# Eight chained layers on one core: edge tokens moved into the first query block, pieces placed between score passes, the two heads' probability tiles side by side, and one block of the last FFN beside the attention

## The chip, the cores and the metric

The kernel runs on one NeuronCore of a Trainium2 chip, as one launch. The metric is the time of that launch on the device in microseconds (us). Matrix products run on TensorE (PE in the profile, with its weight loads as PEld), sums, maxima and reads of PSUM on VectorE (DVE), activations on ScalarE (ACT), some elementwise work on GpSimd (POOL), and SyncE (SP) issues the DMAs.

## The reference, cut to what matters

The input is 2048 tokens of width 128. Four attention layers and four FFN layers follow each other, each as `x = x + f(layernorm(x))`:

```python
x = x + _L0_attn_ref(...)   # 16 heads of 8, softmax over all 2048 tokens
x = x + _L0_ffn_ref(...)    # 512 wide, gelu
x = x + _L1_attn_ref(...)   # 16 heads of 64, softmax over all 2048 tokens
x = x + _L1_ffn_ref(...)    # silu(x wg) * (x wu), 384 wide
x = x + _L2_attn_ref(...)   # each token sees its left and right neighbour and itself, in a ring
x = x + _L2_ffn_ref(...)    # 8 experts, the best one
x = x + _L3_attn_ref(...)   # a memory of two 32x32 matrices, updated in chunks of 64 tokens
x = x + _L3_ffn_ref(...)    # 8 experts of 176, the best two, and a shared one
```

Three things in this matter for the change. The second attention (L1) needs a row maximum and a row sum over 2048 keys for every query and head. The third (L2) needs the key and value of the neighbours of each token, so a block of 256 tokens needs one token of each neighbouring block. The fourth (L3) is sequential: each of its 32 chunks of 64 tokens starts from the state that the chunk before it left.

## The kernel before

The work stands in two long stretches and an end.

The first stretch is the L0 attention, with the L0 FFN and the keys and values of L1 worked in. The change leaves its order alone.

The second is the L1 attention (`l1_attn`, line 1070 on). Its 2048 queries are cut into five query blocks, `QB`, each as (first token, tokens, columns): 512, 384, 512, 384 and 256 tokens. For each block there are eight pairs of heads; a block and a pair make a **unit**, 40 units in all, worked in the order of the blocks. A unit goes over 16 key tiles of 128 keys. One key tile is: four score passes for each of the two heads (a product with the high part of q, one with its low part, one with the low part of the keys, one that adds the negative row maximum), the exponential of both heads' scores on ACT into tiles `P`, and the product of `P` with the values, which comes one key tile late. The sums over keys are not taken from TensorE: `do_sum` adds up the tiles `P`, on POOL (`acg`) for key tiles 0 to 13 and on DVE (`acd`) for 14 and 15, each head by itself, and `do_merge` adds the two. At the end of the unit `u_end` sums these over the partitions, takes the reciprocal, scales, and after every second pair multiplies with Wo (`stage_wo`). Row maxima of later units are made ahead of time (`u_max`): products of q tiles with 512 keys (`km`), reduced on DVE (`mx`).

The layers after L1's attention run as **pieces** beside it. Each stage is a generator that yields between pieces: `stage_a` (L1 FFN), `stage_a2` and `stage_b` (L2 attention), `stage_b2` (L2 FFN), `stage_c`, `chunk` and `stage_d` (L3 attention), `stage_g`, `stage_e0`, `s_lane` and `stage_e1` (L3 FFN). They work on blocks of 256 tokens, eight in all; `c` and `d` on 128, `chunk` on 64. L3's FFN has 13 groups of hidden units for each block of 256, so 104 groups. A planner (`Part.may`, `fill`, line 176 on) decides while the program is written, by a cost for each instruction, which piece can go in; `fill` is called twice for each key tile. The result is one fixed order for each engine. What a yield says matters: an integer over 0 asks for so many PSUM banks, "T" says that the piece begins with a product on TensorE; with `only="t"` `fill` takes neither of these kinds.

`stage_b` of any block waits for `stage_m`, which carries three single **edge tokens** (1280, 1792 and 2047) through the L1 FFN. They ride as extra columns in the second query block, `(512, 384, 388)`, and so come out with unit 15. `stage_a` of a block waits for the query block that holds it.

The third stretch, here the **end**, is what the pieces have left when the 40 units are done. Five more lanes for the FFN are opened there, and all remaining banks. L3's FFN adds its 13 groups for a block up in one PSUM bank, `ac`, which it holds from `stage_e0` to `stage_e1`.

Of the kernel before, what the change touches and what calls it, by code (L numbers as in the profile page):

```python
# [20 lines left out]
D = 128  # L21
# [10 lines left out]
T = dict(lead0=22, more0=4, mgap=0.4, pvq=2, lim0=0.5, fq=(3,), pl=-0.5, pr=1.0, tlow=2, tback=3, late=0.3, pvp="mx", mxp="mx", ex=(1280, 1792, 2047), low=1, lows='ge', keep=1, leave=2, pvn=1, sp=0, rdy=40., eu=2, qg=(22, 16, 10), em=2, el=6, sem=0.2, same=1.2, tsame=3.0, order="hdmBbAaEcCeg", ps=dict(st=3, mx=5), dma=2.3, slack=0.1, lim=0.3, backlog=2.5, lead=(10, 8, 6), pp=7, dve=(14, 15), qp=(1, 1), lanes=2, xl=5,  # L32
         QB=[(0, 512, 512), (512, 384, 388), (896, 512, 512), (1408, 384, 384), (1792, 256, 256)])

# [36 lines left out]
def body(ctx: ExitStack, tc: tile.TileContext, x, pa, pb, pc, pi, pd, pr, pr0, pe, pw, out):  # L71
# [90 lines left out]
    pp = ctx.enter_context(tc.tile_pool(name="pp", bufs=T["pp"]))  # L162
# [31 lines left out]
    class Part:  # L194
# [24 lines left out]
        def step(self):  # L219
            piece[0] = clk["T"]  # L220
            r = next(self.gen, "end")
            self.same = r == "same"
            self.ready = 0.0 if self.same else piece[0] + (r if type(r) is float else 0.0)
            self.pe = r == "T"
            self.banks = r if type(r) is int else 0
            self.seen = len(emitted) if r is False else -1
            if r == "end":
                emitted.add(self.key)
            return r != "end"
# [140 lines left out]

    QB = T["QB"]
    EXTRA = T['ex']
    units = [(qb, p) for qb in range(len(QB)) for p in range(NP1)]
    qhh, qfs, kmx, mx1 = {}, {}, {}, {}

    qx = [mid.tile([128, 8], F32R, name=f"qx{i}") for i in range(2)]
    xq = {}

    def u_loadx(qb):
        t0, tn, n = QB[qb]  # L380
        xq[qb] = l1x.tile([128, 512], F32, name="xq", tag="xq", bufs=2)
        if n != tn:
            ge.memset(xq[qb][:, tn:n], 0.0)
            for i, t in enumerate(EXTRA):
                sy.dma_start(xq[qb][:, tn + i:tn + i + 1], xnd[:, t:t + 1])
        sy.dma_start(xq[qb][:, :tn], xnd[:, t0:t0 + tn])

    def u_qprep(u):
        qb, p = units[u]
        if qb not in xq:  # L390
            u_loadx(qb)
        n = QB[qb][2]
        yield 1
        ps = mi()
        mm(ps[:, :n], C("wq", p * 128, 128), xq[qb][:, :n])
        yield
        qf = l1x.tile([128, 512], F32, name="qf", tag="qf")
        se.activation(qf[:, :n], ps[:, :n], AF.Identity, bias=bq8[:, p:p + 1], scale=0.125)
        rel(ps)
        yield  # L400
        qhh[u] = l1q.tile([128, 512], F32R, name="qh", tag="qh")
        se.copy(qhh[u][:, :n], qf[:, :n])
        yield
        qfs[u] = qf
        tn, n = QB[qb][1:]
        if n > tn:
            for e in range(2):
                r = slice(64 * e, 64 * e + 64)
                se.copy(qx[u % 2][r, 4 * e:4 * e + n - tn], qf[r, tn:n])
# [15 lines left out]
    def u_max(u, i):  # L425
# [8 lines left out]
        if 128 * qt == tn:  # L434
            ps = amx()
            mm(ps[0:8], qx[u % 2], kmx[(u, c)])
            ve.tensor_reduce(mx1[u][0:8, 0, 3, c:c + 1], ps[0:8], AX.X, ALU.max)
            rel(ps)
            return 1
# [9 lines left out]
    def u_maxend(u):  # L449
# [6 lines left out]
        if n > tn:  # L456
            ve.tensor_reduce(m[0:8, 0, 3:4], mx[0:8, 0, 3, :], AX.X, ALU.max)
        yield 1
        t = mi()
        if n > tn:  # L460
            te.transpose(t[0:1, 256:264], m[0:8, 0, 3:4], ident[0:8, 0:8])
# [5 lines left out]
        if n > tn:  # L467
            for e in range(2):
                se.mul(mbt[u % 2][64 * e:64 * e + 1, tn:n], t[0:1, 256 + 4 * e:256 + 4 * e + n - tn], -1.0)
# [50 lines left out]
    l0w = l0ctx.enter_context(tc.tile_pool(name="l0w", bufs=2))  # L520
    qd = dram.tile([16, 6, 8, S], BF16, name="qd")
# [150 lines left out]
    def l0_attn():  # L672
# [49 lines left out]
        for g in range(N):  # L722
# [9 lines left out]
            for q in range(4):  # L732
# [17 lines left out]
                p = pp.tile([128, 512], F32, name="P", tag="P")  # L750
# [202 lines left out]
    leave[0] = T["leave"]  # L953
# [10 lines left out]
    l1a = ctx.enter_context(tc.tile_pool(name="l1a", bufs=2, reuse_waits="tile"))  # L964
# [11 lines left out]
    def u_end(u, o, accs):  # L976
# [4 lines left out]
        if u == len(units) - 1:  # L981
            for e in range(2):
                mm(t[64 * e:64 * e + 64, :n], ones[:, 0:64], accs[e][:, :n], par=(e == 1))
# [8 lines left out]
        for e in range(2):  # L992
            mm(t[32 * e:32 * e + 32, :n], ones[:, 0:32], accs[e][:, :n], tile_position=(0, 32 * e), par=(e == 1))
# [29 lines left out]
    def stage_wo(qb, part):  # L1023
# [4 lines left out]
        for p in range(2 * part, 2 * part + 2):  # L1028
            mm(ps[:, :n], C("wo", p * 128, 128), O.pop(p)[:, :n], start=(p % 2 == 0), stop=(p % 2 == 1))
            yield  # L1030
        if part == 0:
            w = l1w.tile([128, 512], F32, name="wac", tag="wac", bufs=1)
# [9 lines left out]
        del wacc[qb]  # L1042
        yield 1
# [9 lines left out]
        if n != tn:  # L1053
            ne = len(EXTRA)
            xm = edge_x[0] = sm.tile([ne, 128], F32, name="xm", tag="xm", bufs=1)
            for i, t in enumerate(EXTRA):
                sy.dma_start(xm[i:i + 1, :], xs[t % 128:t % 128 + 1, t // 128, :])
# [8 lines left out]
    def l1_attn():  # L1066
        LEAD = dict(zip((256, 384, 512), T["lead"]))
        LEAD.update({260: LEAD[384], 388: LEAD[512]})
# [13 lines left out]
        def do_pv(g, pts, v):  # L1082
            u, k = divmod(g, 16)
            n = QB[units[u][0]][2]
            if k == 0:
                pv[u] = take([T["pvp"]])
            for e in range(2):
                mm(pv[u][64 * e:64 * e + 64, :n], v[:, k % SPC, 64 * e:64 * e + 64], pts[e][:, :n],
                   start=(k == 0), stop=(k == 15), par=(e == 1))
            if k == 15:  # L1090
# [5 lines left out]
                rel(pv.pop(u))  # L1096
                ends.append((u, o, accs))

        def do_sum(g, pts, v):
            u, k = divmod(g, 16)  # L1100
            n = QB[units[u][0]][2]
            for e in range(2):
                a = acc.setdefault(u, [None, None])
                f = first.setdefault((u, e), {})
                eng, nm = (ve, "d") if k in T["dve"] else (ge, "g")
                if nm not in f:
                    f[nm] = [pts[e]]
                    continue
                if len(f[nm]) == 1:
                    if u:  # L1110
                        need(("s", u - 1), ("o", u - 1))
                    t = l1a.tile([128, 512], F32, name="ac" + nm, tag="ac" + nm)
                    eng.tensor_tensor(t[:, :n], f[nm][0][:, :n], pts[e][:, :n], ALU.add)
                    f[nm] = [t, 1]
                else:
                    t = f[nm][0]
                    eng.tensor_tensor(t[:, :n], t[:, :n], pts[e][:, :n], ALU.add)
                if k == 15:
                    a[e] = f["d"][0]
                    merge.append((f["d"][0], f["g"][0], n))  # L1120
                    del first[(u, e)]
# [3 lines left out]
        def do_merge():  # L1125
            while merge:
                d, g_, n = merge.pop(0)
                ve.tensor_tensor(d[:, :n], d[:, :n], g_[:, :n], ALU.add)
            while ends:
                u, o, accs = ends.pop(0)  # L1130
                helper(("o", u), u_end(u, o, accs), max(wr[tname(t)] for t in accs))
# [4 lines left out]
        for g in range(16 * U):  # L1136
# [6 lines left out]
            if u + 2 < U:  # L1143
                if k == 1 and units[u + 2][1] == 0:
                    need(("q", u + 1))
                    u_loadx(units[u + 2][0])
# [10 lines left out]
            pts = []  # L1157
# [3 lines left out]
            for i, (a, b) in enumerate(ops):  # L1161
                for e in range(2):
                    rows = slice(64 * e, 64 * e + 64)
                    mm(pss[e][:, :n], a[rows], b[rows, :n], start=(i == 0), stop=(i == 3), par=e and 0.02)
            for e in range(2):
                pt = pp.tile([128, 512], F32, name="P", tag="P")
                se.activation(pt[:, :n], pss[e][:, :n], AF.Exp)
                rel(pss[e])
                pts.append(pt)
            max_upto(max_at(g + 16 + LEAD[n] + 1))  # L1170
            fill()
            if prev:
                do_sum(*prev[-1])
            if len(prev) == T["pvn"]:
                while prev:
                    do_pv(*prev.pop(0))
                fill()
            do_merge()
# [135 lines left out]
    def stage_m():  # L1314
# [22 lines left out]
        xt = sm.tile([128, 4], F32, name="xtm", tag="xtm", bufs=2)  # L1337
        yield from norm_T(xt)
        h = sm.tile([128, 12], F32, name="hm", tag="hm", bufs=1)
        for k in range(3):  # L1340
# [4 lines left out]
            th = sm.tile([128, 4], F32, name="thm", tag="thm", bufs=2)  # L1345
# [3 lines left out]
            ve.scalar_tensor_tensor(h[:, 4 * k:4 * k + ne], th[:, :ne], 0.5, ps[:, 64:64 + ne], ALU.mult, ALU.mult)  # L1349
# [3 lines left out]
        for k in range(3):  # L1353
            mm(ps[:ne, :128], h[:, 4 * k:4 * k + ne], tok(wi, 6 + k), start=(k == 0), stop=(k == 2))
# [4 lines left out]
        xt = sm.tile([128, 4], F32, name="xtm", tag="xtm", bufs=2)  # L1359
        yield from norm_T(xt)  # L1360
        ps = mi()
        for i in range(2):
            mm(ps[:, 4 * i:4 * i + ne], tok(w2m, i), xt[:, :ne])
        yield
        for i in range(2):
            for j, t in enumerate(EXTRA):
                se.activation(edge[:, t // BN, i, int(t % BN > 0):int(t % BN > 0) + 1], ps[:, 4 * i + j:4 * i + j + 1],
# [258 lines left out]
    def chunk(b, c):  # L1626
# [49 lines left out]
        yield  # L1676
# [151 lines left out]
    def lane_tiles(lane):  # L1828
# [4 lines left out]
        if lane not in lane_bufs:  # L1833
            n = lane - LANES
            if n < 2:
                t = ("acd", "acg")[n]
                ws = [l1a.tile([128, 512], F32, name=t, tag=t)[:, :384] for _ in range(2)]
# [10 lines left out]
    def lane_work(lane):  # L1848
        if lane < LANES:
            return bt(f"t3{lane}", 1), bt(f"te{lane}", 1)  # L1850
        p = pp.tile([128, 512], F32, name="P", tag="P")
        return p[:, :BN], p[:, BN:]
# [19 lines left out]
    def stage_e0(b):  # L1872
        d = E[b]
        yield 1
        ac = mi()
        for i in range(BT):
            mm(tok(ac, i), tok(d["rT"][:, 0], i), pes[0:9, 128:256], start=(i == 0), stop=False)
        d["ac"] = ac

    def s_lane(lane):  # L1880

        q = []
        while ("l", NB_ - 1) not in emitted:
# [33 lines left out]
            yield T["late"]  # L1917
            d["left"] -= 1
            for i in range(BT):
                mm(tok(ac, i), tok(th[:nr], i), w[:nr, 2, :], start=False, stop=(d["left"] == 0 and i == BT - 1))  # L1920
            if d["left"] == 0:
# [3 lines left out]
    def stage_e1(b):  # L1925
        c0, ac = BT * b, E.pop(b)["ac"]
        add_tok(ac, c0)
        yield
# [69 lines left out]
    def s_e0():  # L1998
        for b in range(NB_):
            yield from wait(("g", b))  # L2000
            if b and not tail:
                yield from wait(("l", b - 1))
# [115 lines left out]
```

## Time and profile before

| | |
|---|---|
| median of three runs | 2989.47 us (2988.46 to 3006.5) |
| the profiled execution | 3001.08 us |
| its span, first to last instruction | 2999.2 us |
| first and last score pass of the L1 attention (PE, `mbt,onr`) | 908.6 and 2593.8 us |
| from there to the end of the span | 405 us |
| PE busy | 2769.9 us (92%) |
| DVE busy | 2194.9 us (73%) |
| ACT busy | 1582.9 us (53%) |
| POOL busy | 1522.3 us (51%) |
| granted TensorE clock, mean | 0.936 |

Busy time is the union of an engine's instructions. PE is counted busy from a matmul's start to its modelled end, so a PE busy to 100% can still have small gaps between its products; weight loads (PEld) lie beside it. Nearly every instruction has the line 147, that of the helper that records it, so the groups are told apart by the tiles that they write and read (out<-in).

### The profile page before, as it was taken

The page shows a single profiled execution, that of the slowest core. Times are in us where ns is not written, and L with a number is a line of the kernel's source. Part 1 is how long each engine was busy: PE and PEld are TensorE (multiplying, and loading weights), DVE is VectorE, ACT ScalarE, POOL GpSimd, SP SyncE. Part 2 cuts the span into 40 slices and gives each one's busy share as a digit, 9 for nine tenths or more (in the row PEclk, how much of TensorE's full clock was granted, in tenths as well). Part 3 has the DMA queues.
Part 4 walks back from the last instruction along what each step waited for, and adds up shares of the span by engine and source line. Part 5 has one row for each costly group of instructions (what it writes and reads, how often), then busy time and mean ns, then how long its engine had stood idle before and what let it go on. Part 6 is the DMA issues. An engine that isn't in the chain of part 4 may idle for free.

```text
span 2999.2 us, 49776 instructions
## 1 busy us (share of the span) xinstructions
PE 2769.9 (92%) x16719; PEld 1307.0 (44%) x16719; DVE 2194.9 (73%) x4699; ACT 1582.9 (53%) x3933; POOL 1522.3 (51%) x1762
## 2 busy tenths in 40 slices
PE   7999999999979899999999999899989898888998
PEld 2222222322234344454444444455544555565666
DVE  7899898898534666566666778887677769787765
ACT  1788887888854444444444444444434334333444
POOL 2400110201127688866776876677767556443444
PEclk9999999999979999999999999999999999776779
DMA  6311231321144333433442332233334343312244
GB/s 142 72 28 22 72 84 17 101 54 46 53 141 135 92 112 110 121 110 111 138 119 87 94 95 87 89 105 108 109 97 114 108 117 94 88 52 61 76 104 115
DMA packets 247749, 275.80 MB, mean 92 GB/s; under 512 B 95747, under 2 KB 183330, under 8 KB 247366
## 3 DMA queue, kind: packets, MB, share of 16 engines
q1 hardware_dynamic: 246630, 272.43, 33.2%
q8 instruction: 132, 2.16, 0.3%
q14 instruction: 123, 1.01, 0.1%
q10 hardware_dynamic: 864, 0.20, 0.0%
HBM read 229.97 MB, written 42.28 MB: 91 GB/s over the span
## 4 chain that ended last, share of the span: by engine, by line
PE 70%; DVE 18%; ACT 6%; issue 3%; DMA 3%; POOL 1%; SPq 0%; ACTq 0%; DVEq 0%; POOLq 0%
PE mi L147 70%; DVE mx L147 5%; ACT P L147 3%; DVE sB L147 1%; DVE o L147 1%; DVE gq L147 1%; DMA ka<-kvd 1%; DVE gt L147 1%; DVE xs L147 1%; ACT kf L147 1%; ACT kh L147 1%; DVE xn L147 1%; DVE sG L147 1%; DVE acd L147 1%; DVE sA L147 0%
## 5 line engine op out<-in xcount | busy, mean ns | idle before, releaser
L147 DVE TENSOR_REDUCE mx<-mi 128x1 f32<-128x512 f32 (+1 forms) x2080 | 1322.1, 683 | 582.8 <-PE mi L147 571.5
L147 ACT ACTIVATE P<-mi 128x512 f32<-128x512 f32 (+3 forms) x2304 | 1137.0, 551 | 1004.1 <-PE mi L147 973.2
L147 POOL TENSOR_TENSOR acg<-acg,P 128x512 f32<-128x512 f32 (+3 forms) x960 | 1011.4, 1083 | 181.8 <-ACT P L147 180.0
L147 PE MATMUL mi<-P,ka 128*64 128x512 f32 (+3 forms) x2560 | 597.6, 546 | 2.3 <-DVE mx L147 2.3
L147 PE MATMUL mi<-qh,ka 64*128 64x512 f32 (+3 forms) x2560 | 521.0, 406 | 9.7 <-DMA ka<-kvd 6.8
L147 PEld LDWEIGHTS mi<-qh,ka 64*128 64x128 f32 x2560 | 247.0, 189 | 382.5 <-issue 347.0
L147 PE MATMUL mi<-kop,qop 48*128 48x512 bf16 x1024 | 348.6, 405 | 24.5 <-DVE mx L147 12.1
L147 PE MATMUL mi<-qop,kop 50*128 50x512 bf16 x1024 | 317.8, 391 | 27.1 <-ACT P L147 24.7
L147 PE MATMUL mi<-P,vop 128*32 128x512 f32 x2048 | 304.3, 623 | 13.9 <-ACT P L147 13.9
L147 POOL TENSOR_SCALAR vep<-mv 128x2 f32<-128x2 f32 (+1 forms) x24 | 5.5, 229 | 495.6 <-DVE mv L147 495.6
L147 PE MATMUL mi<-km,qh 64*128 64x512 f32 x1024 | 225.6, 410 | 30.4 <-DVE mx L147 23.8
L147 PE MATMUL mi<-mbt,onr 64*128 64x512 f32 (+3 forms) x1280 | 228.7, 351 | 1.5 <-DMA mbt<-mb 1.5
L147 PE MATMUL mi<-ql,ka 64*128 64x512 f32 (+3 forms) x1280 | 229.2, 353 | 0.0
L147 PEld LDWEIGHTS mi<-P,ka 128*64 128x64 f32 x2560 | 129.2, 137 | 225.3 <-issue 195.1
L147 PEld LDWEIGHTS <-kop 50*128 50x128 bf16 x1024 | 63.6, 95 | 304.9 <-issue 281.6
L147 POOL TENSOR_TENSOR acg<-P 128x512 f32<-128x512 f32 (+3 forms) x80 | 91.1, 1158 | 202.5 <-DVE acd L147 162.0
L147 PEld LDWEIGHTS mi<-km,qh 64*128 64x128 f32 x1024 | 107.1, 189 | 60.5 <-DVE mx L147 38.5
L147 PEld LDWEIGHTS mi<-mbt,onr 64*128 64x128 f32 x1280 | 124.6, 190 | 13.9 <-DMA mbt<-mb 2.2
L147 PEld LDWEIGHTS mi<-ql,ka 64*128 64x128 f32 x1280 | 125.7, 192 | 0.0
L147 PEld LDWEIGHTS <-qop 48*128 48x128 bf16 x1024 | 72.9, 96 | 97.2 <-issue 82.7
L147 PEld LDWEIGHTS mi<-P,vop 128*32 128x32 f32 x2048 | 55.5, 109 | 119.8 <-issue 90.7
L147 POOL TENSOR_TENSOR kl<-kf,kh 128x512 f32<-128x512 f32 x32 | 40.9, 1278 | 110.9 <-ACT kh L147 82.4
(509 smaller groups left out, 3464.4 us busy)
## 6 DMA issues: line engine op xcount, KB each, us to landing
ka<-kvd SPq DMA_DIRECT2D x320, 384.0 KB
km<-khd SPq DMA_DIRECT2D x159, 256.0 KB
khd<-kh SPq DMA_DIRECT2D x32, 256.0 KB
kvd<-kh SPq DMA_DIRECT2D x32, 256.0 KB
kvd<-kl SPq DMA_DIRECT2D x32, 256.0 KB
kvd<-vt SPq DMA_DIRECT2D x16, 512.0 KB
ka<-in_pw_dram SPq DMA_DIRECT2D x37, 192.0 KB
w3s<-in_pw_dram SPq DMA_DIRECT2D x35, 192.0 KB
```

What stands on the lines that cost most here:

```text
L147: r = f(*a, **k)
```

## The change

- **Edge tokens.** There are five of them (256, 768, 1280, 1792, 2047), they ride in the first query block, `(0, 384, 392)`, and the second block takes 512 tokens. The order of the units becomes: two pairs of the second block, all eight of the first, the other six of the second, then the blocks as before (`SEG`). The edge tokens come out with unit 9. The rows that carry them go from 8 to 16.
- **Pieces between score passes.** `fill(9.0, "t")` is called after each of the first three score passes, after the exponentials and twice around the product with the values. It takes pieces that need neither a bank nor TensorE. The second product of `stage_wo` and a product in `chunk` now say "T".
- **Tiles side by side.** `P`, `acd` and `acg` hold both heads, `[128, 2, 512]`; one instruction adds both. DVE takes key tiles 5, 6, 11 and 12, POOL the others. There are five such tiles `P` instead of seven single ones.
- **One block of the last FFN beside the attention, a bank per group.** Outside of the end, `stage_e0` and each group of `s_lane` take a bank of their own and add it to `xs` with `add_tok`. Block 0 may run so; block 1 and the others wait for the end (`fa=1`).

```diff
-T = dict(lead0=22, ... ex=(1280, 1792, 2047), ... pp=7, dve=(14, 15), ...
-         QB=[(0, 512, 512), (512, 384, 388), (896, 512, 512), (1408, 384, 384), (1792, 256, 256)])
+T = dict(pp1=5, fa=1, ti=(0, 1, 2), tf=1, lead0=22, ... ex=(256, 768, 1280, 1792, 2047), ... pp=7, dve=(5, 6, 11, 12), ...
+         QB=[(0, 384, 392), (384, 512, 512), (896, 512, 512), (1408, 384, 384), (1792, 256, 256)])
...
-            self.pe = r == "T"
+            self.pe = r == "T" or type(r) is float
...
-    units = [(qb, p) for qb in range(len(QB)) for p in range(NP1)]
+    SEG = [(1, 0, 2), (0, 0, 8), (1, 2, 8), (2, 0, 8), (3, 0, 8), (4, 0, 8)]
+    units = [(qb, p) for qb, p0, p1 in SEG for p in range(p0, p1)]
...
-            for e in range(2):
-                a = acc.setdefault(u, [None, None])
-                f = first.setdefault((u, e), {})
-                eng, nm = (ve, "d") if k in T["dve"] else (ge, "g")
...
+            f = first.setdefault(u, {})
+            eng, nm = (ve, "d") if k in T["dve"] else (ge, "g")
+            if nm not in f:
+                f[nm] = [pts]
...
+                t = f[nm][0]
+                eng.tensor_tensor(t[:, :, :n], t[:, :, :n], pts[:, :, :n], ALU.add)
...
             for i, (a, b) in enumerate(ops):
                 for e in range(2):
                     rows = slice(64 * e, 64 * e + 64)
                     mm(pss[e][:, :n], a[rows], b[rows, :n], start=(i == 0), stop=(i == 3), par=e and 0.02)
+                if T["tf"] and i in T["ti"]:
+                    fill(9.0, "t")
+            pts = pp.tile([128, 2, 512], F32, name="P", tag="P")
             for e in range(2):
-                pt = pp.tile([128, 512], F32, name="P", tag="P")
-                se.activation(pt[:, :n], pss[e][:, :n], AF.Exp)
+                se.activation(pts[:, e, :n], pss[e][:, :n], AF.Exp)
                 rel(pss[e])
-                pts.append(pt)
             max_upto(max_at(g + 16 + LEAD[n] + 1))
             fill()
+            if T["tf"]:
+                fill(9.0, "t")
...
+            own = ac is None
+            yield 1 if own else T["late"]
+            if own:
+                ac = mi()
...
+            if own:
+                yield
+                add_tok(ac, BT * b)
...
-            if b and not tail:
-                yield from wait(("l", b - 1))
+            while not tail and b >= T["fa"]:
+                yield False
```

## The prediction

> **What bounds the kernel now.** I read the slices of the page first, to see where TensorE falls short, then the busy time by stretches, cut at the score passes and at the last chunk of the L3 attention, then the groups of instructions, to price what moves.
>
> ```profile
> PE   7999999999979899999999999899989898888998
> DVE  7899898898534666566666778887677769787765
> PEclk9999999999979999999999999999999999776779
> ```
>
> The first 12 slices are the L0 part, the next 22 or so the L1 attention, the last five and a half the end. In the attention PE has a 9 nearly everywhere at full clock; in the end it has 8s at a clock of 0.6 to 0.7.
>
> ```profile
> core 0: us, PE busy (x) PEld busy (x) DVE busy (x) ACT busy (x) POOL busy (x), PEclk, DMA share, GB/s
> 908.50:1284.00 375.50, 366.55 (x2093) 160.87 (x2093) 224.42 (x347) 177.35 (x343) 298.79 (x263) 0.98 0.37 112
> ...
> 1640.00:2594.00 954.00, 893.40 (x5813) 462.41 (x5809) 733.88 (x1573) 405.44 (x1201) 648.34 (x760) 0.95 0.36 102
> 2594.00:2643.00 49.00, 39.17 (x177) 26.34 (x174) 41.89 (x176) 14.44 (x74) 10.52 (x22) 0.73 0.12 36
> 2643.00:2924.00 281.00, 244.70 (x1223) 181.60 (x1223) 205.53 (x793) 110.94 (x492) 119.91 (x210) 0.72 0.30 77
> 2924.00:2999.20 75.20, 61.59 (x335) 49.15 (x333) 42.84 (x105) 35.50 (x97) 37.27 (x49) 0.93 0.49 115
> ```
>
> So the attention is bound by PE: 94 to 98% busy. Whatever is put beside it costs about its own PE time. The end is bound by no one engine: PE 85% at clock 0.76, DVE 72%. There 18 chunks of L3, each waiting for the last, set the pace to 2924 us (the first chunk after 2594 stands at 2631, the last at 2924: 17 us a chunk); then 38 of the 104 FFN groups are left. No FFN group ran before 2643.
>
> **How the work moves.** This is from the program order of both kernels, cut after the last score pass. Chunks after it: 18 before, 10 after. FFN groups after it: 104 and 91. L2 blocks: one in both (block 7, whose tokens are the last query block). TensorE instructions after it: 914 and 652; the sum over the kernel is the same, so 262 go into the attention. A float32 product shows as two records in the trace and a transpose as one, so the end has about 1700 records before and 1233 after, of which 386 stand behind the last chunk, where 336 stood.
>
> **The end.** It has 1731 records in 405 us, 0.234 us each, and the three stretches differ little (0.23 from 2643 to 2924 and 0.23 behind). 1233 x 0.234 = **288 us**, 117 less. What speaks for a steady price: the end starts with FFN work of four blocks ready, so its first 49 us would no longer be empty of it. What speaks against a lower one: block 7 can start only when the attention ends.
>
> ```profile
> L147 ACT COPY oT<-mi x8: 344/344/361, 1735.9 to 2706.8; 8x256 f32<-8x256 f32 x8
> ```
>
> Its router output (the last oT) stands at 2706.8, 113 us behind the attention. Then come a stage c (50 us from its first to its last step in the end of before), four chunks of 12 to 17 us and 75 to 87 us of FFN: 113 + 50 + 56 + 80 = 299 us. That chain is nearly as long as the 288. If it decides, the saving is 106.
>
> **The attention, base.** Units without pieces: 42.9 us for 512 columns (units 1 to 7, by the copies of o on ACT: 949 to 1249 us), 35.6 for 388 (units 11 to 15). That is 0.059 us a column, so 27.8 for 256. 16 x 42.9 + 16 x 35.3 + 8 x 27.8 = 1473 us of the 1685, and 212 us are what 570 product instructions of pieces cost: 0.37 us each, stalls included. 262 more at this price are **+97 us**. The other way, each product at its mean start-to-start time, gives +76. I take +85. The four more columns of 392 cost 8 units x 4 x 0.059 = 2 us, within that. Five narrow loads for edge tokens instead of three, and a second load for the split block, are SP issues of 0.3 to 0.5 us with a unit of lead, except at the start, where unit 2's loads now come in unit 0: 0 to 5 us, taken as 1.
>
> **The sums side by side.** The rows:
>
> ```profile
> L147 POOL TENSOR_TENSOR acg<-acg,P 128x512 f32<-128x512 f32 x384 | 489.7, 1311 | 51.2 <-ACT P L147 51.0
> L147 DVE TENSOR_TENSOR acd<-P 128x512 f32<-128x512 f32 x32 | 20.6, 683 | 0.0
> L147 DVE TENSOR_TENSOR o<-o,rb 128x512 f32<-128x512 f32 x16 | 32.6, 2039 | 0.9 <-DMA rb<-rcd 0.8
> ```
>
> A unit of 512 columns has 26 POOL additions, 34 us of its 43. After it has 11 of 1024: by 256 against 512 columns (738 and 1311 ns) one is 2.46 us, so 27 us. DVE goes from four instructions of 683 ns to four twice as long: by 256 and 512 columns (455 and 683) 1.14 us each, +1.8 us a unit, some 60 to 75 over the 40. None of this is on PE's path while DVE and POOL have room. DVE also takes over some 400 instructions of pieces; at 0.27 us (290 us for 1073 in the end) that is 108. DVE goes from 1186 busy of 1686 to about 1360 of 1770: 77%, and near 90% in the units where L3's stage c is thick. In 1800 to 2000 us it already stood at 86%, and PE still at 94%: I add nothing for it beyond the price of the pieces, which was taken there. The merge now waits for POOL's sum of key tile 15, where POOL's last was 13. That sum ends about when the maxima of the next key tile are through on DVE, so 0 to 1 us a unit on DVE. Behind the merge stand the maxima that free PSUM banks; PE waited only 36 us for those in the whole attention. Five double tiles P hold five key tiles, seven single ones held three and a half, so ACT's 20 us of waiting for acg can only shrink.
>
> One row speaks both ways. Scaling o took 656 ns at best and 2039 on average, 10.9 us at most, and POOL was at work in nearly all the slow ones. The Trainium skill ("SBUF — State Buffer", Who interferes with whom) says that a DVE instruction with two SBUF inputs and a GpSimd one that reads SBUF take a shared port in turns, each for its whole length. By that rule an addition of 2.46 us would hold DVE twice as long at each meeting. By the trace POOL is busy for 71% of the attention and would be for about 60%, and its idle time, 4 us in one piece at a unit's end (162 us waiting for acd), is split over two places in each unit. I count this as nothing; bounds: -20 us, if long waits like the 10.9 go, to +60, if each doubles (the slow instructions with SBUF operands lose some 120 us on DVE now) and half reaches PE.
>
> **More places for pieces.** The new calls take no TensorE work, so the order of the products changes only through the planner. What they do is let a chain step more than twice in a key tile. In the attention a chunk took 29 to 35 us at its best, and 22 chunks are to fit now instead of 14; the edge tokens help, since stage b waits for them no longer than unit 9 instead of 15. If the planner's places don't agree with the true times, each such product stalls PE: that is in the 0.37 us, and worth 0 to +50 us if the thicker packing doubles it.
>
> **Sum.** -117 + 85 = -32. The profiled execution of 3001.1 becomes 2969; the median of the runs shown is 11.6 lower, so 2957 from 2989.5. Little stands against it: of two sums near 100, either one wrong by a third turns it around. About 1% is what a measurement of this kernel tells from no change.
>
> **Rivals.**
> - *A, the forecast:* the end shrinks by 105 to 135, the attention grows by 70 to 95: 2920 to 2965. Chance 0.52.
> - *B, the chain of block 7 decides the end and the pieces cost their full price:* -106 + 97 = -9, so 2980. For it: 113 us until oT, in an end that had no FFN work at first. Against it: those 113 us held L2 pieces behind 18 chunks; now 10. Within 1%. Chance 0.24.
> - *C, slower: DVE becomes the bound in the thick units.* Place: the units of the second and third query blocks, where pieces of L3's stage c, the sums and the maxima meet. DVE's instructions there, at the mean times of before, come to 50 to 60 us for units that take 47 to 53 on PE. It decides where DVE passes 90% of a unit: the maxima come late, banks with them, and PE waits. Some dozen units at 4 to 6 us more, and the port waits doubled, are +60 to +110: -117 + 85 + 85 = +53, so 3042; at the low end 3017. For it: the row of o. Against it: 86% without loss of PE. Chance 0.24.
> - *The change doesn't do what it says:* excluded by the order, as far as places go.
>
> **Range.** From A's low end with fewer port waits, 2905, to C's low half, 3035. Faster by over 1% 0.50, within 1% 0.24, slower 0.26.
>
> **What would show it.** Last score pass at 2670 to 2690 us and 285 to 300 us behind it. PE at 94% or more from 1300 us on. Ten chunks behind the last score pass, the first within 20 us. The additions on POOL at 2.4 to 2.6 us, on DVE at 1.1 to 1.3. Wrong it would be if PE's waiting for mx went from 36 to over 80 us (C), or if block 7's oT came later than 110 us into the end and PE had 7s behind it (B).

## The result, and the profile after

The changed kernel takes 3022.5 us (median of 17 executions, 3007.2 to 3033.8) where the kernel before took 2997.6 on the same chip (2981.3 to 3012.1): a ratio of 1.0082, with a 95% interval of 1.0065 to 1.0100. It is slower by 0.8%; the forecast was 1% faster.

The profiled executions (3001.1 and 3017.0 us) show where the 16 us come from. The score passes now run from 907.0 to 2720.7 us:

| | before | after | forecast |
|---|---|---|---|
| attention, first to last score pass | 1685 | 1814 (+128) | +85 |
| end | 405 | 295 (-111) | -117 |
| chunks of L3 in the end | 18 | 10 | 10 |
| DVE busy in the attention | 1186 (70%) | 1447 (80%) | 1360 (77%) |
| DVE's sums (`acd`) in it | 84 | 233 | 145 to 160 |
| POOL busy in it | 1202 | 1040 | about 60% |

So the end did what was said of it, and the attention grew by 43 us too much. The slices of the page after:

```profile
PE   7998999999979999999999999899999899988888
DVE  7899898898434667787897798989769877888765
PEclk9999999999979999999999998999999899997879
```

DVE, which stood at 5 to 8 through most of the attention, has 7s to 9s from its second block on; the end is down to four slices. Cut at the units (units 16 to 23, the third query block, then the end in two parts), busy time of each engine with its instructions in brackets:

```profile
core 0: us, PE busy (x) PEld busy (x) DVE busy (x) ACT busy (x) POOL busy (x), PEclk, DMA share, GB/s
...
1582.00:2043.00 461.00, 430.96 (x2262) 199.25 (x2264) 387.94 (x702) 189.70 (x467) 255.78 (x162) 0.93 0.28 81
...
2721.00:2926.00 205.00, 172.83 (x870) 128.58 (x871) 153.59 (x568) 78.71 (x314) 83.48 (x144) 0.78 0.31 84
2926.00:3015.30 89.30, 73.90 (x377) 59.60 (x375) 48.20 (x118) 41.87 (x113) 41.80 (x55) 0.87 0.52 117
```

The same units before:

```profile
1544.00:1941.00 397.00, 377.62 (x2074) 170.05 (x2072) 307.90 (x558) 174.33 (x393) 289.64 (x250) 0.98 0.30 92
```

The third block grew by 64 us, half of all that the attention grew by, though it got only 190 more PE records; DVE is busy in it for 84% (78% before), and the granted clock is 0.93 there and not 0.98. In the waits of the attention, each with its sum, number and longest, PE and its weight loads (PEld) stand waiting for DVE's row maxima, `mx`. After:

```profile
PEld mi L147 <- DVE mx L147: 123.5, 151, 4.0
PE mi L147 <- DVE mx L147: 48.0, 42, 3.4
```

and before:

```profile
PEld mi L147 <- DVE mx L147: 83.7, 96, 6.9
PE mi L147 <- DVE mx L147: 36.2, 25, 6.6
```

What made DVE late is in the groups of the attention, forms kept apart (busy time, mean of one in ns, idle time before it). After:

```profile
L147 POOL TENSOR_TENSOR acg<-acg,P 128x1024 f32<-128x1024 f32 x160 | 397.6, 2485 | 261.4 <-ACT P L147 248.1 <-ACT thm L147 2.5 <-ACT dz L147 1.9
...
L147 DVE TENSOR_TENSOR acd<-acd,P 128x1024 f32<-128x1024 f32 x32 | 59.6, 1862 | 0.0
L147 DVE TENSOR_TENSOR acd<-P 128x1024 f32<-128x1024 f32 x16 | 43.7, 2730 | 0.0
```

POOL's addition takes 2.49 us, as forecast (2.46). DVE's takes 1.21 us where POOL has nothing beside it, close to the forecast 1.14, but 1.86 and 2.73 on average. DVE now makes 160 such instructions; at the length that they have alone (1.21, 0.95, 0.95 and 0.67 us by width) they are 160 us, and they took 233.

### The profile page after: what moved, and what is told of

Read it like the earlier page. It is cut to its first block, busy times and chain, and to the rows that moved or that the text cites. A ratio compares the mean times of both kernels' runs of the same rounds, so it can differ in the third digit from the quotient of the medians.

```text
span 3015.3 us, 48031 instructions
## 1 busy us (share of the span) xinstructions
PE 2779.1 (92%) x16719; PEld 1302.0 (43%) x16719; DVE 2366.9 (78%) x4724; ACT 1593.6 (53%) x3927; POOL 1318.1 (44%) x1150
## 4 chain that ended last, share of the span: by engine, by line
PE 58%; DVE 27%; ACT 6%; issue 4%; DMA 3%; POOL 1%; SPq 1%; ACTq 0%; POOLq 0%; DVEq 0%
PE mi L147 58%; DVE mx L147 9%; DVE acd L147 3%; ACT P L147 3%; DVE gt L147 1%; DVE xn L147 1%; DVE o L147 1%; DMA ka<-kvd 1%; DVE sB L147 1%; DVE xs L147 1%; DVE sc L147 1%; ACT kf L147 1%; DMA rb<-rcd 1%; SPq L147 1%; DMA rcd<-rc 1%
## 5 line engine op out<-in xcount | busy, mean ns | idle before, releaser
L147 POOL TENSOR_TENSOR acg<-acg,P 128x1024 f32<-128x1024 f32 (+3 forms) x400 | 814.7, 2037 | 525.7 <-ACT P L147 493.5
L147 PE MATMUL mi<-P,ka 128*64 128x512 f32 (+3 forms) x2560 | 605.6, 552 | 0.5 <-DVE h L147 0.3
L147 PE MATMUL mi<-qh,ka 64*128 64x512 f32 (+3 forms) x2560 | 529.9, 409 | 15.7 <-ACT P L147 9.0
L147 PE MATMUL mi<-km,qh 64*128 64x512 f32 x1024 | 241.8, 418 | 31.1 <-DVE mx L147 22.0
L147 POOL TENSOR_TENSOR acg<-P 128x1024 f32<-128x1024 f32 (+3 forms) x40 | 82.7, 2067 | 76.3 <-ACT P L147 37.0
L147 DVE TENSOR_TENSOR acd<-acd,P 128x1024 f32<-128x1024 f32 (+3 forms) x80 | 109.7, 1371 | 0.2
```

The costliest lines, as they stand in the source:

```text
L147: r = f(*a, **k)
```

## The experiments

Every ratio is to the kernel before on the same chip, with its 95% interval. Attention and end are from one profiled execution each, which can lie some 10 us beside the median, so the ratios decide. Most of the pairs compared below ran on two chips, each beside the kernel before; the pair with nothing moved under the new share ran on one.

The theory at the start (theory 1): POOL's additions of double length hold DVE longer at each meeting, and DVE's late maxima hold PE. The rivals: the calls between score passes pack the pieces too densely; the pieces simply cost more PE time; DVE has too much work, whatever POOL does.

### One part taken away

**Each POOL addition in two instructions, one per head.** Nothing else is touched: the order on PE, DVE, ACT and SP is that of the changed kernel, instruction for instruction.

```diff
+        def add(eng, o, a, b):
+            if eng is ge:
+                for e in range(2):
+                    eng.e.tensor_tensor(o[:, e], a[:, e], b[:, e], ALU.add)
...
-                eng.tensor_tensor(t[:, :, :n], t[:, :, :n], pts[:, :, :n], ALU.add)
+                add(eng, t[:, :, :n], t[:, :, :n], pts[:, :, :n])
```

> The changed kernel with each of POOL's additions of two heads issued as two instructions of one head; the order of everything else is the same, instruction for instruction. If the length for which one POOL instruction holds DVE off is what costs: DVE's acd in the attention falls from 233 to 150-190 us and the median by 15 to 40 us, to 2980-3007. If only POOL's total time matters, or the packing: acd stays at 220-240 us, the median at 3015-3030.

Measured: **0.9927** [0.9901, 0.9953], 2976.1 us. The attention is 1770 us, the end 297. The groups of this kernel's attention:

```profile
L1112 POOL TENSOR_TENSOR acg<-acg,P 128x512 f32<-128x512 f32 x320 | 435.3, 1388 | 196.8 <-ACT P L147 196.6
...
L147 DVE TENSOR_TENSOR acd<-acd,P 128x1024 f32<-128x1024 f32 x32 | 45.1, 1411 | 0.0
...
L147 DVE TENSOR_TENSOR acd<-P 128x1024 f32<-128x1024 f32 x16 | 28.0, 1753 | 0.0
```

POOL needs more time for the same sums (435 against 398 us), and the kernel is 1.5% faster: DVE's first addition falls from 2.73 to 1.75 us. One row of the change, halved in length and doubled in number, turns its sign. DVE's sums fall from 233 to 187 us in the attention, and the time above the shortest of each kind that its other instructions lose (the maxima left out) from 247 to 220.

**The old share: DVE takes key tiles 14 and 15.** Planned anew; 7 chunks in the end.

```diff
-dve=(5, 6, 11, 12)
+dve=(14, 15)
```

> The changed kernel with DVE's share of the sums over keys put back to key tiles 14 and 15; POOL has the other fourteen, both heads in one instruction. In program order 7 chunks and 91 FFN groups stand in the end (10 and 91 in the changed kernel). Theory 1 (the sums moved to DVE meet POOL's, wait, and hold up the maxima): DVE's time on acd in the attention falls from 233 us to 100-130, the attention from 1814 to 1750-1775, the median from 3022 to 2960-2985. Theory 2 (the attention grows because of the pieces put into it, whoever does the sums): three more chunks in the attention, 1815-1830 us, the end some 15 us shorter, the median 3005-3025.

Measured: 1.0077 [1.0053, 1.0102], attention 1858, end 255. The waits in DVE's sums are gone (80 us for the group), but the time is no better, against theory 1, which had said 2960 to 2985 us: the new plan puts still more pieces into the attention, and DVE's other instructions lose 344 us to waits where they lost 247.

**No calls between score passes.** 17 chunks and all FFN groups are back in the end.

```diff
-tf=1
+tf=0
```

> The changed kernel without the calls of fill between and behind the score passes (tf=0), all else as changed. In program order 17 chunks and 104 FFN groups stand in the end, nearly as before (18 and 104). Theory 1: the attention keeps the cost of the sums, 1730-1750 us, the end is 390-400 us again, the median 3030-3060. Theory 2: the attention is as before, 1685-1700 us, the end 390-400, the median 2985-3005.

Measured: 1.0131 [1.0105, 1.0156], attention 1753, end 377. It is slower than the whole change, so the calls are not the loss.

**The tiles side by side alone:** old query blocks (the second with 392 columns, where the kernel before has 388), old order of the units, old share, no calls, no FFN beside the attention.

```diff
-fa=1, tf=1, ex=(256, 768, 1280, 1792, 2047), dve=(5, 6, 11, 12)
+fa=0, tf=0, ex=(1280, 1792, 2047), dve=(14, 15)
-QB=[(0, 384, 392), (384, 512, 512), ...]
+QB=[(0, 512, 512), (512, 384, 392), ...]
-SEG = [(1, 0, 2), (0, 0, 8), (1, 2, 8), ...]
+SEG = [(0, 0, 8), (1, 0, 8), ...]
```

> One part alone: the tiles of both heads side by side, one addition for both, with the old share (DVE key tiles 14 and 15), the old query blocks and order of units, three edge tokens, no calls of fill between score passes, no FFN block beside the attention. 18 chunks and 104 FFN groups in the end, as before. Theory 1 puts the cost into the share and the meetings: with POOL's additions twice as long the meetings cost 0 to +25 us, the median 2990-3020. Theory 2: no cost without more pieces, 2985-3000.

Measured: 0.9917 [0.9890, 0.9945], 2970.2 us, attention 1695, end 378, faster than both theories had said. POOL's additions are of double length here too, and nothing is lost. So length alone isn't it.

### Length, share, and both

**POOL's additions in four instructions,** same order as the changed kernel.

```diff
+            if eng is ge:
+                for i in range(4):
+                    e, h = divmod(i, 4 // 2)
+                    w = o.shape[2] * 2 // 4
...
+                    eng.e.tensor_tensor(o[:, e, c], a[:, e, c], b[:, e, c], ALU.add)
```

> The changed kernel with each of POOL's additions issued as four instructions of half a head's columns; PE, DVE, ACT and SP have the same instructions in the same order as in the changed kernel and in the one with halves. If DVE's waits shrink with the length of one POOL instruction: acd in the attention from 187 us (halves) to 160-175, the attention from 1770 to 1745-1760, the median 2950-2968. If halves have taken all there is and POOL's fixed cost for each instruction begins to count: the attention 1765-1785, the median 2974-2995.

Measured: 0.9911 [0.9888, 0.9934], attention 1780. Within the intervals it is no better than two: POOL is busy with its additions for 897 us when they are whole, for 991 in halves and for 1128 in quarters.

**The old share in the order of the changed kernel.** The planner still counts the new share, so that the order on PE and ACT is that of the changed kernel, and only the additions of key tiles 5, 6, 11, 12 and 14, 15 change their engine.

```diff
-            eng, nm = (ve, "d") if k in T["dve"] else (ge, "g")
+            eng, nm = (ve, "d") if k in (14, 15) else (ge, "g")
```

> The changed kernel with the sums of key tiles 5, 6, 11 and 12 back on POOL and those of 14 and 15 on DVE, whole additions of both heads, while the planner still reckons with the new share: PE and ACT keep every instruction in its place, DVE loses two additions a unit. If DVE's time with acd is what holds PE up: acd from 233 to 80-95 us, the attention from 1814 to 1745-1765, the median 2955-2975. If it is the length of POOL's additions alone, whoever waits: the waits move to DVE's other instructions, the attention 1795-1820, the median 3005-3025.

Measured: 0.9999 [0.9984, 1.0013], attention 1810, end 291. It gains 0.8%, half of what the halves gain, and theory 1 had expected more. DVE's sums are down to 80 us, but its other instructions, the maxima left out, lose more: summed over the attention, their time above the shortest of each kind rises from 247 to 309 us. In that the rival was right: the time is the one that it gave.

**Halves under the old share,** in three orders: the replanned one, the tiles alone, the kept order (each the kernel above with POOL's additions in two).

> The kernel with DVE on key tiles 14 and 15 (3021 us, 7 chunks in the end) with POOL's additions issued as two instructions of one head, same order otherwise. If the length of POOL's additions is what its attention of 1858 us pays for (its DVE loses 345 us to waits outside of the sums): these fall to 200-260, the attention to 1785-1815, the median 2945-2980. If the packing alone does it: 1840-1860, the median 3005-3022.

> Tiles side by side alone (2970 us) with POOL's additions issued as two instructions of one head, same order otherwise: what the kernel before did, in the order that the new tiles gave. If the length costs here too, where the attention is less full: the attention from 1695 to 1675-1688, the median 2952-2965. If DVE has room enough there: 1690-1697, the median 2966-2974.

> The sums of key tiles 5, 6, 11 and 12 back on POOL, 14 and 15 on DVE, and POOL's additions as two instructions of one head; PE and ACT in the order of the changed kernel. Against the changed kernel (1.0082 of before), halves alone gave 0.9927 and the share alone 0.9999. If both remove the same thing (DVE's additions meeting POOL's): 0.990-0.997, the attention 1760-1785 us. If the two add up: 0.980-0.988, the attention 1735-1755. If POOL, with 14 of 16 key tiles again, keeps DVE's other instructions waiting as it did in the kernel with that share planned: 0.997-1.005, the attention 1785-1815.

Measured: 1.0094 [1.0069, 1.0119] against 1.0077; 0.9917 [0.9888, 0.9945] against 0.9917; 1.0064 [1.0040, 1.0088] against 0.9999. Halves bring nothing under the old share. Once they seem to cost 0.65%, for which no run here gives the cause; the two kernels ran on different chips, and their profiled executions differ by 3 us only (3009.7 and 3012.7 in span). The waits in DVE's other instructions fall there as well (309 to 284 us in the kept order), without a gain in time; so what halves win under the new share goes with the sums.

**Halves without the calls,** and **halves without the FFN block** (`fa=0`).

> Halves, but no calls of fill between and behind the score passes; 17 chunks and 104 FFN groups in the end. It was 1.0131 with whole additions. If the calls pay for themselves once the additions are short: 0.998-1.006, the attention 1705-1730 us and the end 370-395. If the pieces that they bring in cost what they save: 0.988-0.997.

> Halves, but no FFN block beside the attention; 11 chunks and 104 FFN groups in the end, 1380 records of PE there for 1233. At 0.234 us a record the end is 320-335 us for 297, at 0.37 us a product instruction the attention 1735-1750 for 1770: 0.988-0.998 of before, no difference that matters. If a bank for each group and 13 more additions on DVE cost more than that: 0.980-0.988.

Measured: 0.9948 [0.9929, 0.9967], attention 1703, end 373; and 0.9916 [0.9888, 0.9944], attention 1760, end 304. Against 0.9927 with both parts, the calls are worth 0.2% and the FFN block nothing, both within the intervals.

**Halves with the old query blocks,** the old order of the units and three edge tokens, all else as changed.

```diff
-ex=(256, 768, 1280, 1792, 2047), QB=[(0, 384, 392), (384, 512, 512), ...]
+ex=(1280, 1792, 2047), QB=[(0, 512, 512), (512, 384, 392), ...]
-SEG = [(1, 0, 2), (0, 0, 8), (1, 2, 8), ...]
+SEG = [(0, 0, 8), (1, 0, 8), ...]
```

> Halves, with the old query blocks and order of units and three edge tokens; 11 chunks and 96 FFN groups in the end (10 and 91 with the new blocks). By the price of the pieces the attention is 15-25 us shorter and the end 15-20 us longer than with the new blocks: 0.988-0.998 of before, where 0.9927 was measured. If the new blocks pack the pieces of the later layers less thickly and so save stalls: 0.998-1.008.

Measured: **0.9865** [0.9834, 0.9896], 2957.4 us, attention 1739, end 306. It beats both kernels, by 1.35% the one before, and both forecasts (0.988 at best). The second block has 392 columns here too. The slices of its page:

```profile
PE   7999999999989999999999999999999899988888
DVE  7899888898534766676677888886799878877855
```

### The pair of share and length by itself

Left open was whether new share and double length lose by themselves, or only where the new blocks and the moved pieces crowd the units. Three more runs: the last kernel with whole additions; the new share alone with nothing moved (`fa=0, tf=0`, old blocks, old order), whole and in halves.

> This is the version with the old query blocks, the old order of the units and three edge tokens, but with everything else of the change, and POOL's additions whole. It differs from the run with the same blocks and the additions in two instructions (0.9865) in the length of POOL's additions alone. Theory 1 (a POOL addition of double length, taken up four times a unit beside DVE's additions of double length, holds DVE for its whole length; the blocks and the fills only decide how much room is left): 1.3 to 1.9% slower than that run, so a ratio of 0.999 to 1.006, the attention 30 to 50 us longer than its 1739. Rival R (the loss needs the second query block behind unit 7, where the new blocks put the pieces with the thick units): at most 0.5% slower, a ratio of 0.986 to 0.992.

> The tiles side by side with the new share of the key tiles (DVE 5, 6, 11, 12), whole POOL additions; old query blocks, no calls between score passes, no FFN block beside the attention. The same with the old share (DVE 14, 15) was 0.9917. Theory 1: the share and the length together cost even without any piece moved: a ratio of 1.002 to 1.010, the attention 30 to 50 us longer than 1695. Rival R (it takes the moved pieces to make the waits harmful, since here DVE is as idle as before): 0.990 to 0.995.

> As the run before it in this list, with each POOL addition as two instructions, one per head, and the same order elsewhere. Theory 1: 0.985 to 0.993, 1 to 1.8% faster than with whole additions. Rival R: the same as with whole additions within 0.4%.

Measured: 0.9987 [0.9968, 1.0006] against 0.9865 in halves; 1.0073 [1.0051, 1.0095] against 0.9932 [0.9907, 0.9956]. Whole additions cost 1.2 and 1.4%. Theory 1 had said 1.3 to 1.9 and 1.0 to 1.8, the rival 0.5 and 0.4 at most, so the first comes out just under theory 1's range and the second inside it, and both lie far from the rival. With nothing moved the attention grew less than it had said, by 24 us over the tiles alone and not 30 to 50. The row also answers the rival of too much work on DVE: in halves, the new share (0.9932) costs within the intervals nothing against the old (0.9917). All pairs together; in each pair the order on PE, DVE, ACT and SP is the same:

| DVE's key tiles | moved | POOL whole | POOL in halves | whole costs |
|---|---|---|---|---|
| 5, 6, 11, 12 | the whole change | 1.0082 | 0.9927 | +1.6% |
| 5, 6, 11, 12 | all but the calls | 1.0131 | 0.9948 | +1.8% |
| 5, 6, 11, 12 | all, old query blocks | 0.9987 | 0.9865 | +1.2% |
| 5, 6, 11, 12 | nothing | 1.0073 | 0.9932 | +1.4% |
| 14, 15 | all, replanned | 1.0077 | 1.0094 | -0.2% |
| 14, 15 | all, order kept | 0.9999 | 1.0064 | -0.6% |
| 14, 15 | nothing | 0.9917 | 0.9917 | 0 |

Why the share decides can be read in the run with the new share and nothing moved. In its timeline, first DVE, then POOL (start, length, group):

```profile
1007.80 1.29 DVE L147 TENSOR_REDUCE mx<-mi 128x1 f32<-128x512 f32 x2 [0.96 <-PE mi L147]
1009.01 3.31 DVE L147 TENSOR_TENSOR acd<-P 128x1024 f32<-128x1024 f32 x1
1012.24 2.47 DVE L147 TENSOR_REDUCE mx<-mi 128x1 f32<-128x512 f32 x4
```

```profile
1008.86 8.12 POOL L147 TENSOR_TENSOR acg<-acg,P 128x1024 f32<-128x1024 f32 x3 [4.18 <-ACT P L147]
```

POOL had waited 4.18 us for a tile `P` and starts 0.15 us before DVE's addition. DVE's then lasts 3.31 us: until POOL's first of the three, of 2.38 us, is through, and 1.1 us more. Four maxima follow it without a gap; they had to wait. This repeats in unit after unit: all 16 such additions of the kernel met POOL, and the groups show a price of 2.0 us each time, near to one POOL addition. Whole:

```profile
L147 DVE TENSOR_TENSOR acd<-P 128x1024 f32<-128x1024 f32 x16 | 52.1, 3257 | 0.1
```

In halves:

```profile
L147 DVE TENSOR_TENSOR acd<-P 128x1024 f32<-128x1024 f32 x16 | 26.8, 1673 | 0.1
```

Under the old share the two don't meet. DVE adds at the unit's end while POOL stands and waits for it, as the timelines of the tiles-alone kernel show:

```profile
1031.70 1.22 DVE L147 TENSOR_TENSOR acd<-P 128x1024 f32<-128x1024 f32 x1
1033.02 1.23 DVE L147 TENSOR_TENSOR acd<-acd,acg 128x1024 f32<-128x1024 f32 x1
```

```profile
1034.39 2.38 POOL L147 TENSOR_TENSOR acg<-P 128x1024 f32<-128x1024 f32 x1 [7.34 <-DVE acd L147]
```

POOL's idle time for `acd`, which the forecast saw only as idle time to be "split over two places", was what kept the two apart. On the page before, and then on that after:

```profile
L147 POOL TENSOR_TENSOR acg<-P 128x512 f32<-128x512 f32 (+3 forms) x80 | 91.1, 1158 | 202.5 <-DVE acd L147 162.0
```

```profile
L147 POOL TENSOR_TENSOR acg<-P 128x1024 f32<-128x1024 f32 (+3 forms) x40 | 82.7, 2067 | 76.3 <-ACT P L147 37.0
```

That late maxima carry the loss to PE shows in the weight loads' waits for `mx`: 124 us against 107 in halves for the whole change, 112 against 81 with nothing moved, 105 against 77 with the old query blocks. Under the old share halves don't lower them: 119 and 124 replanned, 111 and 111 in the kept order, 70 and 70 with nothing moved. With nothing moved, whole and in halves, the new share first and then the old:

```profile
PEld mi L147 <- DVE mx L147: 111.7, 137, 4.3
PEld mi L147 <- DVE mx L147: 80.9, 100, 4.2
```

```profile
PEld mi L147 <- DVE mx L147: 70.3, 92, 5.3
PEld mi L147 <- DVE mx L147: 70.3, 88, 5.1
```

One more rival is the granted clock, since executions with a lower one are longer. In the pair with nothing moved it is excluded: at one and the same mean clock of 0.939 the executions take 3018 and 3019 us whole and 2980 in halves. In the other three pairs of the new share the whole additions have a mean clock that is lower by 0.003 to 0.005; at 33 us for 0.015, as among the executions of the changed kernel with halves, that is 7 to 11 of their 31 to 53 us (an estimate).

### The parts of the 0.8%

The ratios add up. Tiles side by side and new share, with whole additions and nothing moved: +0.7% (tiles alone -0.8%). The calls and the FFN block with the old query blocks: 1.0073 to 0.9987 whole, 0.9932 to 0.9865 in halves, so -0.9 and -0.7%. The new query blocks, edge tokens and order of the units on top: 0.9987 to 1.0082 and 0.9865 to 0.9927, so +1.0 and +0.6%. Together +0.8%. By engines, with the halves: moving all of it (from "nothing" to "the whole change") lengthens the attention from 1667 to 1770 and shortens the end from 393 to 297. That is +103 against -95.

## Why the prediction was wrong, point by point

- **The end: right, but its price by luck.** 870 + 377 = 1247 records stand behind the last score pass (1233 forecast), at 295 / 1247 = 0.236 us (0.234 forecast). Ten chunks, as said. But the clock granted in the end was 0.81, where it had been 0.76: a record took more of PE's work (busy time times clock: 0.161 us for 0.152), and the clock made up for it.
- **"The sums side by side ... I count this as nothing": the step that failed.** Tiles and share with nothing moved measured +0.7%, 22 us, where 0 was counted. Under it lies the cost of whole additions beside the new share, 1.2 to 1.8% in four pairs, 46 us in the changed kernel: inside the bound of +60 that the step itself gave, and by the longer waits that it gave as the reason. The value was taken from how much of the time POOL is busy, which did fall (71 to 57%). What matters is whether the two engines add at the same moment, and the change took away the place where they did not. The row for it was at hand: 162 us of POOL waiting for `acd`. The rule cited there, of a shared port held for a whole instruction, fits what the runs show: 3.26 us for 1.21, 1.67 with halves. The same section of the Trainium skill ("SBUF — State Buffer", Who interferes with whom) says that reductions never contend; here `mx` took 682 ns with no POOL instruction beside it and 679 with one for most of its time.
- **The price of moved pieces, +85: right only in sum.** With halves the attention is +85, but that is -18 for tiles and sums and +103 for the 459 records, about 250 products, that move between those two kernels: some 0.41 us a product and not 0.37. The end gave 95 for them. The forecast's gain of 32 from moving was not there; with the old query blocks about 20 to 26 of it was.
- **"Four more columns ... 2 us" and "0 to 5 us, taken as 1" for the query blocks: the second term that failed.** They cost 0.6 to 1.0% with the calls, 18 to 28 us. Units 0 to 15 took 664 us with them and 626 without, in halves, and the third block 443 and 422; the fourth gave 22 back and the end 9. Which of edge tokens, order and sizes does it was not tried apart, so this cause stays open. The forecast was -32 us and +25 came: with whole additions the sums account for 22 of the difference, the query blocks for some 25, and the rest of the move for the last 9 or so.
- **DVE's load: too low for the reason above.** 1447 us and not 1360; 73 of the 87 us are the sums' own waits.
- **Rival B** can't be told apart by the end's length: its 299 us and the forecast's 288 lie on both sides of the 295. Its own sign, an oT of block 7 later than 110 us into the end, didn't come: the last stands at 2823.2, 102 us in.

```profile
L147 ACT COPY oT<-mi x8: 344/361/363, 1460.4 to 2823.2; 8x256 f32<-8x256 f32 x8
```

- **Rival C was the nearest,** in place (third query block), in mechanism (port waits, then late maxima) and in its low end (3017). Its threshold of 90% told nothing: DVE is busy for 84% of that block with whole additions and, 18 us shorter, for 84% with halves. Nor did its sign: PE's own wait for `mx` went from 36 to 48 us, far from 80; the weight loads' wait, which rose by 40, is the row that should have been named. PE's busy share told nothing either: from 1300 us on it was 94%, as forecast, though the last score pass came at 2721 us and not by 2690.
- **Forecast A's range** doesn't follow from its own bounds: the end shorter by 105 to 135 and the attention longer by 70 to 95 make 2924 to 2979, not 2920 to 2965.

**Open:** why the old share in the changed order gains only 0.8% and nothing from halves, though DVE's sums meet POOL no more there. POOL has more to add there (1025 against 897 us), which may be what holds DVE's other instructions; no run isolates it. The tiles alone shorten the end by 27 us, with the same 18 chunks and 104 groups behind the last score pass. The row of the end before, and then that with the tiles alone (busy time and instructions of PE, PEld, DVE, ACT and POOL, then the granted clock):

```profile
2594.00:2999.20 405.20, 345.46 (x1731) 257.08 (x1727) 290.25 (x1073) 160.88 (x662) 167.71 (x280) 0.76 0.31 79
```

```profile
2602.00:2979.90 377.90, 317.51 (x1705) 237.44 (x1701) 283.06 (x1036) 159.67 (x647) 166.39 (x275) 0.81 0.33 85
```

PE is busy for 28 us less, and its busy time times the clock is nearly the same (262 and 259 us), so the gain goes with a higher granted clock; why more was granted is open.

## What to carry to other kernels

Before an addition is given to another engine, look for what keeps the two engines apart now: idle time of one "until" the other is done can be what makes both fast. Where two engines hold each other up, as here, the price of a meeting is about the other's whole instruction, so short instructions on the engine off the critical path can pay for the time that they add there; here they did so only where the two met. And work moved from a stretch of mixed limits into one that is bound by TensorE was close to a zero sum here (+103 against -95 us), so small terms set the sign.

## What the runs showed of the hardware

- A meeting costs both sides: the POOL addition that followed DVE's in the timeline above took 3.24 us instead of 2.38, while DVE's took 3.31 instead of 1.21.
- More and shorter POOL instructions cost it about 0.2 us of busy time each: (991 - 897) / 440 = 0.21 for halves, (1128 - 991) / 880 = 0.16 for quarters, waits for DVE included.
- Executions of one and the same kernel follow the mean granted clock: with halves, 2959 us at 0.955 and 2992 at 0.940.
